# Separate score products for the first four samples, wv fetched last, and part of wk through GpSimd's queue, in a kernel of four graph layers

## The chip, the cores and the metric

The kernel runs on one core of one Trainium2 chip. The metric is the device time of one execution in microseconds (us), taken as the median of several runs; lower is better. The core's engines are named in the profile as PE (TensorE, matrix products), PEld (TensorE's weight loads), DVE (VectorE), ACT (ScalarE), POOL (GpSimd) and SP (SyncE, which issues most DMAs). Each engine executes its own instructions in order; waits between engines go by semaphores. Besides SP, ScalarE and GpSimd can issue DMAs too, each through a queue of its own.

## The reference

Everything is f32. The input is a batch of 128 samples, each of 128 nodes with 512 features, and one weighted adjacency matrix of 128 x 128 a sample. Four graph layers follow each other, each added to its input and normalised. The change lies in the first (layer 0), a diffusion over three hops with attention weights:

```python
x, adj = ...                      # [128, 128, 512], [128, 128, 128]
def L0(X, A, Wv, bv, aw, ab, Wk, bk):          # Wk: three hops, [3, 512, 512]
    Xw = X @ Wv + bv
    sj = Xw @ aw[:512, 0]
    si = Xw @ aw[512:, 0]
    e = leaky_relu(sj[:, None, :] + si[:, :, None] + ab[0], 0.2)
    alpha = A * exp(e)
    transition = alpha / (sum(alpha, -1, keepdims=True) + 1e-12)
    H, Xk = 0, X
    for k in range(3):
        H = H + Xk @ Wk[k] + bk[k]
        Xk = einsum('bij,bjd->bid', transition, Xk)
    return relu(H)
x = layernorm(x + L0(x, adj, ...))
x = layernorm(x + L1(...)); x = layernorm(x + L2(...)); x = layernorm(x + L3(...))
```

Layers 1 to 3 (hypergraph convolution through 1024 features, dense graph layer, masked attention with 8 heads) are not touched.

## The kernel before

**How it is put in order.** The body of the kernel doesn't issue instructions. Each call on `pe`, `ve` (VectorE), `ac` (ScalarE), `po` (GpSimd) or `sp` is recorded by `Plan.add` with a key (`plan.key`, the place wanted), an estimated duration (`estimate`, line 124) and its dependences. `Plan.order` (239) then plays the five engines' queues forward with these estimates, choosing at each step among the operations that could start; it has a model of the DMA path (`LANES` transfers outstanding on SP, a common `pipe`), of buffers that come free, and of the port that VectorE and GpSimd share (`shares_port`, 151). `Plan.emit` (370) does this three times, the later times with due times from `deadlines` (359), and issues everything in the planned order. So every instruction in the profile carries line 381, and groups are told apart by engine, operation and tile name. A change of a key or of one estimate can move any instruction of any engine.

**Layer 0.** `layer0` (990) handles four samples in one call, as two pairs. They are loaded (`from_dram`, tile `four`), transposed on VectorE (`turned_two`, giving `xT`), and `lefts` (809) forms the sums of blocks of `xT` on GpSimd that serve as left operands. `twice` (846) multiplies by the weights with two levels of a Strassen-Winograd scheme: seven outer steps, each a `strassen` (630) of seven products, 49 products in all for the four samples. The seven weight tiles `WT["0"]` have the name `w7`, which the profile shows as `first` together with other tiles that share the space. Each tile holds seven blocks of 128 x 386: 3 x 128 columns for the three hops, and two further columns with Wv times the two halves of `aw`, so that a product yields both the hops' inputs and the attention scores s_j and s_i (`QW = 3 * P + 2`). Results are drained from PSUM banks into `R` (tile `out`) by ScalarE and VectorE. From the two score columns of `R` the softmax is made (key `WHENT[0]`): transposes by TensorE, Prelu and Exp on ScalarE, product with `adj` on VectorE; its result `e` goes through DRAM and comes back transposed, and the two diffusion products (tile `t`) and the normalisation follow (key `WHENT[1]`). The result is written to DRAM as `x1d`.

**The start.** `prepare0` (898) makes the seven weight tiles once. It fetches `aw`, `wv` (two loads of four 128 KB DMAs on SP), the first half of the columns of `wk` for the three hops in two parts (chunks of rows `low` and `high`, on ScalarE's queue and, for two hops of `high`, on SP's), the small vectors, and the second half of `wk` on SP. TensorE broadcasts `aw` to all partitions; VectorE takes eight dot products with the rows of `wv` (`dot`, tiles `junk` and `cols0`), which are the score columns `two`. ScalarE copies the parts of `wk` and the score columns into the blocks of four tiles (B11, B21, B12, B22). `combine`, `combine_apart` and `combine_once_more` (509 to 531) form the sums of blocks and of tiles that the scheme needs, on VectorE with PSUM as one operand (`held_in_bank`, tiles `t0`, `t1` and `bank`) or on GpSimd:

```python
scores = W[j][:, :4, 0, 3 * P:]
if half:
    po.memset(scores, 0.0)
else:
    po.memset(scores[:, 2:], 0.0)
    ac.copy(scores[:, :2], two[:, 2 * g:2 * g + 2])
plan.key = COMBINE[half][g]
(combine_apart if j in (B12,) else combine)(W[j])
```

At the end it makes `c0` (the constant of the scores, from `aw_sum` and `bv_c`), the bias of the hops from `bk`, and leaves a copy of the bias in the PSUM tiles `t0` and `t1`.

Of the kernel before, what the change touches and what calls it, by code (L numbers as in the profile page):

```python
# [14 lines left out]
OP = mybir.AluOpType  # L15
AX = mybir.AxisListType

P = 128
# [25 lines left out]
LAG1, LAG2 = 1, 1.5  # L44
COMBINE = (-9, -2), (-.5, -.2), .1
SOFT = .2
PARKED, LATE = .95, 4
# [126 lines left out]
class Plan:  # L174
# [64 lines left out]
    def order(self, urgent=None):  # L239
# [41 lines left out]
        def look(e):  # L281
# [32 lines left out]
        while count < n:  # L314
# [16 lines left out]
            if o[7]:  # L331
                end = pipe = max(pipe, t + BEGIN) + o[7]
                landed += [end + LANDED] * len(o[1])
                landed = landed[-LANES:]
            if e == PE and o[8] > reached:
# [54 lines left out]
def kernel(  # L390
# [73 lines left out]
    def four():  # L464

        return tile_of("four", U, D)
# [36 lines left out]
    def held_in_bank(kind, block):  # L503

        p = tile_of(kind, QW)
        ac.copy(p, block)
        return p
# [24 lines left out]

# [365 lines left out]
    def prepare0():  # L898
        h = D // 2
        plan.key = -9.7  # L900
        awr = four().rearrange("p u f -> p (u f)")
        sp.dma_start(awr[:1], aw.rearrange("f o -> o f"), run=2 * D, parts=1)
        W = WT["0"] = [tile_of("w7", 7, 1, QW, place=(B11, B21, T2, T1, B22, T3, N4).index(k)) for k in range(7)]
        stage = [W[T2 + m].rearrange("p j o f -> p (j o f)")[:, :C * D].rearrange("p (c f) -> p c f", f=D)
                 for m in range(3)]

        def fetch(queue, dst, src, chunks, columns, run):
# [9 lines left out]

        low, high, every = slice(0, 2), slice(2, 4), slice(0, 4)
        st = [four() for _ in range(2)]
        for g, chunks in enumerate((low, high)):  # L920
            plan.key = -9.7 + .2 * g
            fetch(sp, st[g], wv0, chunks, slice(0, D), D)
        plan.key = -9
        for m in range(3):
            fetch_part(ac, m, low, 0)
        awc, bvc = fixed(2 * C, name="aw_c"), fixed(C, name="bv_c")
        ab_b, bk0b = fixed(1, name="ab_b"), row()
        with plan.together():
            for c, v, n in ((awc, aw, 2 * C), (bvc, bv0, C)):
                ac.dma_start(c, bass.AP(tensor=v.tensor, offset=v.offset, ap=[[1, P], [P, n]]), run=1)  # L930
            ac.dma_start(bk0b[:3], bk0, parts=3)
            ac.dma_start(ab_b, rows(ab, 1), run=1)
# [4 lines left out]
        awb = [bank() for _ in range(2)]  # L937
        for k in range(2):
            pe.matmul(awb[k], ones[:1], awr[:1, k * D:(k + 1) * D], start=True, stop=True)
        two = fixed(C, 2, name="cols0")  # L940
        for c in range(C):
            for k in range(2):
                dot(two[:, c, k:k + 1], st[c // 2][:, c % 2], awb[k])
        plan.key = WHEN0[0] + .05
        for m in range(3):
            fetch_part(sp, m, every, 1)
        plan.key = -9
        for g, half, j in ((0, 0, B11), (1, 0, B21), (0, 1, B12), (1, 1, B22)):
            for m in range(3):
                ac.copy(W[j][:, :4, :, m * P:(m + 1) * P].rearrange("p (n c) o i -> p c n (o i)", n=2),  # L950
                        stage[m].rearrange("p c (n i) -> p c n i", i=P)[:, 2 * g:2 * g + 2, 2 * half:2 * half + 2])
            scores = W[j][:, :4, 0, 3 * P:]
            if half:
                po.memset(scores, 0.0)
            else:
                po.memset(scores[:, 2:], 0.0)
                ac.copy(scores[:, :2], two[:, 2 * g:2 * g + 2])
            plan.key = COMBINE[half][g]
# [3 lines left out]
        combine_once_more(W)  # L962
        plan.key = -9
        p = bank()
# [7 lines left out]

        p = bank()
        pe.matmul(p, ones[:3], bk0b[:3], start=True, stop=True)
        p = p.rearrange("p (h n i) -> p h n i", h=2, n=2)
        ac.copy(bias[:, 0], p[:, 0])
        ve.tensor_tensor(bias[:, 1], p[:, 1], bias[:, 0], OP.subtract)
        plan.key = WHENT[0][0] - .1
        for kind in ("t0", "t1"):
# [10 lines left out]
    def layer0(i0):  # L990
# [16 lines left out]
        def fresh(bs):  # L1007
            def takes(d):
# [9 lines left out]

        twice(left, WT["0"], QW, lambda r, half: [R[r][:, b, 2 * half + n] for b in range(U) for n in range(2)],
              lambda r, half: [R[r][:, b, 2 * half:2 * half + 2] for b in range(U)],  # L1020
              [fresh(bias[:, half]) for half in range(2)], .28)
        yield
# [577 lines left out]
```

## Time and profile before

| what | us |
|---|---|
| median of four runs | 5377.01 |
| the four runs | 5374.19 to 5378.59 |
| the profiled execution's own time | 5374.19 |
| its span in the profile | 5372.4 |
| TensorE busy in it | 5304.7 |
| VectorE, GpSimd, ScalarE busy | 4421.8, 3909.4, 2408.9 |

The span is the time from the first to the last recorded instruction of one execution; 1.8 us lie around it. Busy times are sums of instructions' durations, and an engine that is busy for nearly the whole span, as TensorE is, need not be working at its full rate: a row of TensorE can be a product that goes slowly. The mean granted clock of TensorE over this span was 0.999 of full speed. The page's list of queues gives 806.60 MB to the queue of SP and 1.06 MB to that of ScalarE. The GpSimd queue moves nothing in the kernel before.

In answers to queries, a row of the timeline gives the start, the time it covers, the engine, line, operation, tiles (out<-in), shape and count, and in brackets the idle time ahead of it with what ended it.

### The profile page before, as it was taken

To read this page: it belongs to the slowest core of one execution; us is meant where nothing else is said; L and a number is where in the kernel's file an instruction comes from. 1 tells how busy PE (TensorE), PEld (TensorE's weight loads), DVE (VectorE), ACT (ScalarE), POOL (GpSimd) and SP (SyncE) were. 2 spreads that over 40 slices of the span, in tenths; PEclk is the share of its full clock that TensorE was granted. 3 is DMA by queue.
4 is the path that set the end of the run, shared out by engine and by line. 5 is a ranking of instruction groups with operands and counts; after the bars stand their busy time and mean duration, and the time that the engine had idled before them with its cause. 6 is when DMAs were issued, how large, how long until landed. Compare 5 with 4: busy or idle time off the path is not lost.

```text
span 5372.4 us, 92973 instructions
## 1 busy us (share of the span) xinstructions
PE 5304.7 (99%) x29039; PEld 4226.1 (79%) x29039; DVE 4421.8 (82%) x11721; ACT 2408.9 (45%) x6085; POOL 3909.4 (73%) x4937
## 2 busy tenths in 40 slices
PE   8999999999999999999999999999999999999998
PEld 4555555555888888888888889988998898889897
DVE  7788887887888888888888778888887888788776
ACT  3343343343544444444444344444444444444444
POOL 6777787676766666666666577777877777778776
PEclk9999999999999999999999999999999999999999
DMA  4444555445544554444444745555555455545543
GB/s 109 142 136 132 147 137 137 120 117 189 167 143 147 159 162 143 147 159 160 143 148 152 235 141 163 157 160 152 162 159 160 152 163 158 163 152 163 156 153 111
DMA packets 831143, 813.61 MB, mean 151 GB/s; under 512 B 258348, under 2 KB 631604, under 8 KB 830648
## 3 DMA queue, kind: packets, MB, share of 16 engines
q1 hardware_dynamic: 827650, 806.60, 49.1%
q8 instruction: 231, 3.78, 0.3%
q14 instruction: 264, 2.16, 0.1%
q10 hardware_dynamic: 2998, 1.06, 0.1%
HBM read 458.38 MB, written 349.04 MB: 150 GB/s over the span
## 4 chain that ended last, share of the span: by engine, by line
PE 87%; DVE 7%; issue 2%; DMA 1%; POOL 1%; ACT 1%; SPq 0%; ACTq 0%; DVEq 0%; POOLq 0%
PE bank L381 66%; PE t L381 21%; DVE four L381 2%; DVE out L381 1%; DVE col L381 1%; DVE junk L381 1%; DVE first L381 1%; POOL out L381 0%; SPq L381 0%; ACT out L381 0%; DVE side L381 0%; DVE rows L381 0%; POOL four L381 0%; ACT four L381 0%; DMA four<-x 0%
## 5 line engine op out<-in xcount | busy, mean ns | idle before, releaser
L381 PE MATMUL bank<-first,four 128*128 128x386 f32 (+3 forms) x6352 | 1746.9, 422 | 23.2 <-ACT first L381 9.6
L381 PEld LDWEIGHTS bank<-first,four 128*128 128x128 f32 (+2 forms) x6352 | 1088.4, 186 | 599.7 <-DVE out L381 102.5
L381 DVE TENSOR_TENSOR out<-bank,out 128x386 f32<-128x386 f32 (+1 forms) x1942 | 949.6, 508 | 249.6 <-PE bank L381 193.7
L381 DVE TENSOR_TENSOR four<-bank,four 128x256 f32<-128x256 f32 x1113 | 455.1, 417 | 150.9 <-PE bank L381 138.8
L381 POOL TENSOR_TENSOR out<-out 128x772 f32<-128x772 f32 (+3 forms) x249 | 341.8, 1383 | 271.9 <-DVE out L381 212.0
L381 POOL TENSOR_TENSOR four<-four 128x256 f32<-128x256 f32 (+2 forms) x434 | 352.1, 824 | 186.6 <-DVE four L381 140.0
L381 PE MATMUL bank<-first,out 128*128 128x256 f32 (+1 forms) x1746 | 432.3, 377 | 3.8 <-DVE four L381 1.6
L381 POOL TENSOR_TENSOR four<-four,four 128x256 f32<-128x256 f32 (+2 forms) x467 | 397.5, 856 | 10.0 <-PE bank L381 1.5
L381 POOL TENSOR_TENSOR col<-col,neghalf 128x2 f32<-128x2 f32 x320 | 228.6, 715 | 231.3 <-DVE col L381 229.6
L381 ACT COPY out<-bank 128x258 f32<-128x258 f32 (+2 forms) x489 | 195.2, 404 | 437.3 <-PE bank L381 365.2
L381 PEld LDWEIGHTS bank<-first,out 128*128 128x128 f32 (+1 forms) x1746 | 318.5, 188 | 65.4 <-issue 9.0
L381 ACT ACTIVATE four<-four,col,col 128x512 f32<-128x512 f32 (+1 forms) x355 | 308.5, 892 | 125.7 <-POOL col L381 119.9
L381 DVE TENSOR_TENSOR first<-bank,first 128x256 f32<-128x256 f32 (+1 forms) x591 | 240.8, 416 | 98.6 <-PE bank L381 89.1
L381 PE MATMUL bank<-first 128*128 128x128 f32 (+1 forms) x2132 | 297.4, 277 | 1.6 <-DVE four L381 1.6
L381 DVE BATCH_NORM_STATS2 col<-four 128x6 f32<-128x512 f32 x424 | 283.3, 682 | 10.5 <-ACT four L381 9.1
L381 ACT COPY four<-bank 128x256 f32<-128x256 f32 (+1 forms) x358 | 150.8, 424 | 302.2 <-PE bank L381 291.5
L381 PEld LDWEIGHTS bank<-first 128*128 128x128 f32 (+1 forms) x2132 | 269.7, 189 | 15.8 <-issue 3.8
L381 PE MATMUL t<-out,sq 128*128 128x512 f32 x512 | 256.3, 593 | 0.5 <-ACT t L381 0.5
L381 ACT COPY t<-out 128x512 f32<-128x512 f32 x256 | 150.9, 591 | 235.0 <-PE bank L381 83.7
L381 PE MATMUL t<-first,four 128*128 128x256 f32 (+2 forms) x1064 | 249.7, 360 | 0.6 <-DVE four L381 0.6
L381 PE MATMUL bank<-out,first 128*128 128x128 f32 (+3 forms) x1432 | 232.5, 312 | 2.2 <-DVE col L381 1.8
L381 PE MATMUL bank<-four,first 128*128 128x128 f32 (+3 forms) x1400 | 220.5, 303 | 2.4 <-DVE four L381 1.3
(526 smaller groups left out, 13154.7 us busy)
## 6 DMA issues: line engine op xcount, KB each, us to landing
h<-four SPq DMA_DIRECT2D x69, 512.0 KB, 3.3
four<-in_x_dram SPq DMA_DIRECT2D x256, 128.0 KB, 3.4
four<-h SPq DMA_DIRECT2D x64, 512.0 KB, 4.9
four<-in_x_dram SPq DMA_DIRECT2D x62, 512.0 KB, 4.6
x1d<-four SPq DMA_DIRECT2D x62, 512.0 KB, 2.9
four<-x1d SPq DMA_DIRECT2D x60, 512.0 KB, 4.6
out<-h SPq DMA_DIRECT2D x55, 512.0 KB, 5.1
h<-out SPq DMA_DIRECT2D x50, 512.0 KB, 3.2
```

What stands on the lines that cost most here:

```text
L381: call(*map(real, args), **{n: real(a) for n, a in kw.items()})
```

## The change

The kernel's three products for the hops keep their form, but the start is rearranged:

- `prepare0` fetches `bk` first. The first half of `wk` goes by chunks: the `low` ones on ScalarE's queue, the `high` ones on GpSimd's, as twelve DMAs of 64 KB. The second half stays on SP. `aw`, `wv` and the tiny vectors get the key `SCORE0` = .8 and follow on SP; `wv` is put into tiles `prep`. The broadcasts of `aw`, the eight dots and `c0` get that key too. The bias is made early.
- `WT["0"]` is filled and combined over its first 384 columns only. `score_columns` later adds the two score columns of all 49 blocks: small sums on GpSimd, copies on ScalarE.
- For the first four samples, `layer0` multiplies with 384 columns, and the scores come from 16 products of `xT` with the two columns `two`, in one bank, copied to `R` by ScalarE. The softmax of these samples gets a key not before `SCORE0 + .2`. All later samples are computed as before, with 386 columns.
- In the planner, a DMA issue on GpSimd is estimated at 1000 ns, doesn't claim the shared port, and doesn't count among SP's outstanding transfers.

```diff
@@ estimate, shares_port, order
-        return ISSUE
+        return 1000 if engine == POOL else ISSUE
-        return name != "memset"
+        return name not in ("memset", "dma_start")
-                if e == SP:
+                if ops[k][7] and e != POOL:
...
@@ weights
-        p = tile_of(kind, QW)
+        p = tile_of(kind, 3 * P)
...
-        flat = [w.rearrange("p j o f -> p (j o f)") for w in W]
         for to, a, b in ((T3, T2, B11), (N4, B21, T2)):
-            for at in (slice(0, 4 * QW), slice(4 * QW, 7 * QW)):
-                po.tensor_tensor(flat[to][:, at], flat[a][:, at], flat[b][:, at], OP.subtract)
+            for at in (slice(0, 4), slice(4, 7)):
+                po.tensor_tensor(W[to][:, at, 0], W[a][:, at, 0], W[b][:, at, 0], OP.subtract)
+
+    def score_columns(W, two):
+
+        last = lambda j: W[j][:, :, 0, 3 * P:]
+        sc = fixed(3, 7, 2, name="cols7")
+        po.memset(sc, 0.0)
+        for j in (B22, T3):
+            po.memset(last(j), 0.0)
+        for k in range(2):
+            top, low = two[:, 2 * k], two[:, 2 * k + 1]
+            ac.copy(sc[:, k, B11], top)
+            ac.copy(sc[:, k, T2], top)
+            ac.copy(sc[:, k, B21], low)
+            po.tensor_tensor(sc[:, k, T1], sc[:, k, T3], top, OP.subtract)
+            po.tensor_tensor(sc[:, k, N4], low, top, OP.subtract)
+        po.tensor_tensor(sc[:, 2], sc[:, 1], sc[:, 0], OP.subtract)
+        for j, k in ((B11, 0), (B21, 1), (T2, 0), (N4, 2)):
+            ac.copy(last(j), sc[:, k])
+        po.tensor_tensor(last(T1), last(T3), sc[:, 0], OP.subtract)
@@ prepare0
-        for m in range(3):
-            fetch_part(ac, m, low, 0)
...
-        for m in range(3):
-            fetch_part(sp if m else ac, m, high, 0)
+        for g, chunks in enumerate((slice(0, 2), slice(2, 4))):
+            plan.key = -9
+            for m in range(3):
+                fetch_part((ac, po)[g], m, chunks, 0)
+        plan.key = WHEN0[0] + .05
+        for m in range(3):
+            fetch_part(sp, m, slice(0, 4), 1)
...
+        plan.key = SCORE0
+        awr = prep()
+        sp.dma_start(awr[:1], aw.rearrange("f o -> o f"), run=2 * D, parts=1)
+        st = [prep().rearrange("p (u f) -> p u f", f=D) for _ in range(2)]
+        for g in range(2):
+            fetch(sp, st[g], wv0, slice(2 * g, 2 * g + 2), slice(0, D), D)
...
+        two = WT["cols"] = fixed(C, 2, name="cols0")
@@ layer0
+        wide = QW if i0 else 3 * P
+        twice(left, [w[:, :, :, :wide] for w in WT["0"]], wide,
...
+        if not i0:
+            two = WT["cols"]
+            plan.key = base + SCORE0 + .1
+            pt = bank()
+            with plan.together(30):
+                for r in range(2):
+                    for b in range(U):
+                        at = 2 * (U * r + b)
+                        for c in range(C):
+                            pe.matmul(pt[:, at:at + 2], xT[r][:, b, c], two[:, c], start=r == b == c == 0,
+                                      stop=c == C - 1, skip_group_check=True)
+            for r in range(2):
+                ac.copy(R[r][:, :, 0, 3 * P:], pt[:, 2 * U * r:2 * U * r + 2 * U].rearrange("p (b k) -> p b k", k=2))
+            score_columns(WT["0"], two)
+            plan.key = base
...
-            plan.key = base + WHENT[0][r]
+            plan.key = base + (WHENT[0][r] if i else max(WHENT[0][r], SCORE0 + .2))
```

In the order that the planner makes of the changed kernel, the engines' instructions differ from those of before at the start and, in places, through layer 0; after the last layer-0 samples the orders are the same.

More of the change, by code (lines that the diff above doesn't have):

```diff
@@ L45 @@
 COMBINE = (-9, -2), (-.5, -.2), .1
+SCORE0 = .8
 SOFT = .2
@@ L332, in order @@
                 end = pipe = max(pipe, t + BEGIN) + o[7]
-                landed += [end + LANDED] * len(o[1])
-                landed = landed[-LANES:]
+                if e != POOL:
+                    landed += [end + LANDED] * len(o[1])
+                    landed = landed[-LANES:]
             if e == PE and o[8] > reached:
@@ L900, in prepare0 @@
         plan.key = -9.7
-        awr = four().rearrange("p u f -> p (u f)")
-        sp.dma_start(awr[:1], aw.rearrange("f o -> o f"), run=2 * D, parts=1)
+        bk0b = row()
+        sp.dma_start(bk0b[:3], bk0, parts=3)
         W = WT["0"] = [tile_of("w7", 7, 1, QW, place=(B11, B21, T2, T1, B22, T3, N4).index(k)) for k in range(7)]
@@ L905, in prepare0 @@
                  for m in range(3)]
+        W = [w[:, :, :, :3 * P] for w in W]
         def fetch(queue, dst, src, chunks, columns, run):
@@ L916, in fetch_part @@
             fetch(queue, stage[m][:, at[0], at[1]], wk0[m], *at, h)
[L918 to L922, printed above, removed]
-        plan.key = -9
-        for m in range(3):
-            fetch_part(ac, m, low, 0)
[L926 to L932, printed above, removed]
-        for m in range(3):
-            fetch_part(sp if m else ac, m, high, 0)
+        for g, chunks in enumerate((slice(0, 2), slice(2, 4))):
[5 more added lines that the diff above has]
+            fetch_part(sp, m, slice(0, 4), 1)
+        plan.key = -9
         ones = fixed(P, name="ones")
         po.memset(ones, 1.0)
[L937 to L947, printed above, removed]
+        p = bank()
+        pe.matmul(p, ones[:3], bk0b[:3], start=True, stop=True)
+        p = p.rearrange("p (h n i) -> p h n i", h=2, n=2)
+        ac.copy(bias[:, 0], p[:, 0])
+        ve.tensor_tensor(bias[:, 1], p[:, 1], bias[:, 0], OP.subtract)
         for g, half, j in ((0, 0, B11), (1, 0, B21), (0, 1, B12), (1, 1, B22)):
@@ L951, in prepare0 @@
                         stage[m].rearrange("p c (n i) -> p c n i", i=P)[:, 2 * g:2 * g + 2, 2 * half:2 * half + 2])
[L952 to L957, printed above, removed]
             plan.key = COMBINE[half][g]
@@ L962, in prepare0 @@
         combine_once_more(W)
-        plan.key = -9
+        plan.key = SCORE0
[4 more added lines that the diff above has]
+            fetch(sp, st[g], wv0, slice(2 * g, 2 * g + 2), slice(0, D), D)
+        awc, bvc = fixed(2 * C, name="aw_c"), fixed(C, name="bv_c")
+        ab_b = fixed(1, name="ab_b")
+        with plan.together():
+            for c, v, n in ((awc, aw, 2 * C), (bvc, bv0, C)):
+                sp.dma_start(c, bass.AP(tensor=v.tensor, offset=v.offset, ap=[[1, P], [P, n]]), run=1)
+            sp.dma_start(ab_b, rows(ab, 1), run=1)
+        awb = [bank() for _ in range(2)]
+        for k in range(2):
+            pe.matmul(awb[k], ones[:1], awr[:1, k * D:(k + 1) * D], start=True, stop=True)
+        two = WT["cols"] = fixed(C, 2, name="cols0")
+        for c in range(C):
+            for k in range(2):
+                dot(two[:, c, k:k + 1], st[c // 2][:, c % 2], awb[k])
         p = bank()
@@ L971, in prepare0 @@
         ve.tensor_tensor(c0, p[:, :1], ab_b, OP.add)
[L973 to L978, printed above, removed]
+        plan.key = SCORE0
         for kind in ("t0", "t1"):
@@ L1017, in fresh @@
             return takes
-        twice(left, WT["0"], QW, lambda r, half: [R[r][:, b, 2 * half + n] for b in range(U) for n in range(2)],
-              lambda r, half: [R[r][:, b, 2 * half:2 * half + 2] for b in range(U)],
+        wide = QW if i0 else 3 * P
+        twice(left, [w[:, :, :, :wide] for w in WT["0"]], wide,
+              lambda r, half: [R[r][:, b, 2 * half + n, :wide] for b in range(U) for n in range(2)],
+              lambda r, half: [R[r][:, b, 2 * half:2 * half + 2, :wide] for b in range(U)],
               [fresh(bias[:, half]) for half in range(2)], .28)
+        if not i0:
[6 more added lines that the diff above has]
+                        at = 2 * (U * r + b)
+                        for c in range(C):
+                            pe.matmul(pt[:, at:at + 2], xT[r][:, b, c], two[:, c], start=r == b == c == 0,
[4 more added lines that the diff above has]
+            plan.key = base
         yield
```

## The prediction

> **What bounds the kernel now.** I read the page's busy shares and slices first, then the stretches of the first 70 us, then the instructions of TensorE and of the engines that release it, then the transfers.
>
> ```profile
> PE 5304.7 (99%) x29039; PEld 4226.1 (79%) x29039; DVE 4421.8 (82%) x11721; ACT 2408.9 (45%) x6085; POOL 3909.4 (73%) x4937
> ...
> PE   8999999999999999999999999999999999999998
> ```
>
> Over the whole span TensorE is the bound. Only the first slice (134 us) is below 9. In the order of the changed kernel, every engine's instructions are those of before again once the layer-0 samples are through, so what can move lies in the start-up, and in small differences of order in layer 0. The stretches of the start (columns: window, length, then busy us and count of PE, PEld, DVE, ACT, POOL, then clock, DMA share, GB/s):
>
> ```profile
> 0.00:10.00 10.00, 7.51 (x14) 3.43 (x14) 0.16 (x1) 0.31 (x1) 1.06 (x13) 1.00 0.67 147
> 10.00:20.00 10.00, 0.40 (x2) 0.37 (x2) 4.84 (x12) 5.54 (x10) 2.82 (x4) 1.00 0.79 205
> 20.00:30.00 10.00, 7.41 (x17) 3.12 (x17) 9.49 (x24) 5.91 (x15) 3.60 (x3) 1.00 1.14 209
> 30.00:40.00 10.00, 6.62 (x18) 2.72 (x17) 9.35 (x17) 5.09 (x12) 10.00 (x14) 1.00 0.87 150
> 40.00:50.00 10.00, 9.24 (x20) 3.48 (x20) 9.21 (x24) 5.65 (x14) 9.57 (x12) 0.83 0.20 52
> 50.00:60.00 10.00, 9.68 (x24) 5.00 (x24) 4.21 (x10) 1.12 (x3) 10.00 (x6) 0.83 0.11 20
> 60.00:70.00 10.00, 10.00 (x31) 5.41 (x30) 7.87 (x17) 3.58 (x7) 9.92 (x9) 1.00 0.26 74
> ```
>
> Until 30 us the transfers run at their ceiling, from 20 to 50 us VectorE is full, from 30 us on GpSimd. TensorE's busy time flatters: it issues 14 to 24 records in 10 us where it issues 31 once dense. Its own rows:
>
> ```profile
> 19.64 2.94 PE L381 MATMUL bank<-first,four 128*128 128x386 f32 x4 [9.60 <-ACT first L381]
> 28.42 5.73 PE L381 MATMUL bank<-first,four 128*128 128x386 f32 x16 [0.30 <-DVE out L381]
> 38.37 0.92 PE L381 MATMUL bank<-first,four 128*128 128x386 f32 x2 [2.37 <-DVE first L381]
> 50.20 8.44 PE L381 MATMUL bank<-first,four 128*128 128x386 f32 x20
> ```
>
> The first weight product starts at 19.64, released by ScalarE's copy of the score columns. All product rows of this view up to 58.6 us sum to 68 records, 34 products; at a dense 0.65 us each that is 22 us of work. So some 31 us of the start are lost to TensorE, and that is all that this change can touch. What releases it:
>
> ```profile
> 6.17 1.87 PE L381 MATMUL bank<-bv_c,aw_sum 128*128 128x1 f32 x8
> 16.43 0.65 DVE L381 SCALAR_TENSOR_TENSOR junk<-four,bank 128x512 f32<-128x512 f32 x1
> 16.59 1.41 POOL L381 TENSOR_TENSOR four<-four 128x256 f32<-128x256 f32 x2 [14.96 <-DVE four L381]
> 26.40 1.28 POOL L381 TENSOR_TENSOR four<-four 128x512 f32<-128x512 f32 x1 [6.91 <-DVE four L381]
> 30.18 1.14 ACT L381 COPY first<-first 128x512 f32<-128x512 f32 x2
> 46.37 6.34 POOL L381 TENSOR_TENSOR first<-first 128x1544 f32<-128x1544 f32 x2 [0.43 <-DVE first L381]
> ```
>
> To be seen: the dots on wv (16.43 is the first of eight), the operand sums of GpSimd that wait for VectorE's transposes, the last copy of wk's second half at 30.18, and the long combinations from 46.37. The transfers, 0 to 8 us and 8 to 28 us:
>
> ```profile
> DMA packets 3292, 0.98 MB, mean 122 GB/s; under 512 B 1872, under 2 KB 3284, under 8 KB 3292
> ```
> ```profile
> DMA packets 4831, 4.24 MB, mean 212 GB/s; under 512 B 660, under 2 KB 4323, under 8 KB 4831
> ...
> first<-in_L_gnn_Wk_dram SPq DMA_DIRECT2D x12, 128.0 KB, 4.3
> first<-in_L_gnn_Wk_dram ACTq DMA_DIRECT2D x6, 64.0 KB, 2.5
> ```
>
> Twice the size takes nearly twice as long to land, so what counts is bytes, not the issuing queue.
>
> **The change, part by part** (us on the end; minus is gain).
>
> 1. wv out of the front. Ahead of the end of wk's second half stand today two x loads, wv and wk: 5.0 MiB, 5.24 MB, which agrees with 0.98 + 4.24 MB by 28 us. Without wv it is 4.19 MB. At 212 GB/s, 1.05 MB are 4.9 us. The tiny loads (aw_c, bv_c, ab, 4 bytes a piece, most of the 1872 small packets) leave the front too: 0.6 more, since 0.98 MB are worth 4.6 us at 212 GB/s and took 8. Value -5.5. Ends: at the 175 GB/s of 12 to 16 us the 4.19 MB end at 3.4 + 23.9 = 27.3, -0.8; at the 234 of 16 to 20 us they end at 21.3, -6.8.
>
> 2. The eight dots. Each is 0.68 + 0.08 (read of the accumulator), 6.1 in all. Today four of them run from 16.43, four from 22.02. In the new order the first stands three combinations before the end of wk's combining and the rest among the drains of the products that follow, and TensorE's next six products each wait for a drain. VectorE is idle 5.8 us of 50 to 60: cost between 0 (cover holds) and 6.1. Most of the products behind them wait, so +4.
>
> 3. Sixteen score products with 2 columns. Nearest is the 1-column row: 1.87 / 8 = 0.234 a record, at a time when a 512-column record took 0.85 against 0.43 later, so 0.117 at full rate; two records a product. 32 x 0.117 = 3.7; at the slow rate 7.5; 0 if all fall into pauses. They stand in TensorE's order before the last product of their outer step and the softmax, so +3.7. The granted clock was 0.83 in 40 to 60 us. [...]
>
> 4. The broadcasts of aw (3.75 us, four records) and c0 (1.87) go from TensorE's idle start to between its products. Pauses there (2.37 before 38.37) hide them: 0; without that cover 2.8 at full rate.
>
> 5. 384 for 386 columns: 49 products x 2 records x 2 columns x 0.84 ns = -0.2.
>
> 6. Twelve 64 KB loads on GpSimd. Not in the trace. From below the same load on ScalarE's queue, 0.44 an issue; from above 2.5, if each held the queue until it landed. Behind them wait the operand sums, at 16.59 today; GpSimd is free from 1.5 us, so up to (16.6 - 1.4) / 12 = 1.27 an issue they cost nothing. Nearest is 0.44: 0. If the cover is gone, 12 us for each us above 1.27. [...]
>
> 7. Score columns of the weights: six small sums on GpSimd (0.2 each by the col row, 0.72 by the power row) and ten copies of 0.19 on ScalarE ahead of two output sums: 0 to 3, +0.5.
>
> 8. The softmax of the first pair started at 44.10 and its first t product at 65.9, 21.8 later. Now it starts behind the scores, near 56, while TensorE has 22 products (14 us) ahead of that t product. GpSimd's and the DMA part overlap only partly: 0 to 3, +1.
>
> Sum: -5.5 + 4 + 3.7 + 0 - 0.2 + 0 + 0.5 + 1 = +3.5. The profiled execution took 5374.2 (span 5372.4 and 1.8 around it), so 5377.7 on that scale; the median of the runs is 2.8 above it: **5380**. About 0.2% (10.8 us) is what a measurement here can tell from no change, so the likeliest case is no change. All ends together: -7.0 to +21.5, 5370 to 5398.
>
> **The rivals.**
>
> *Faster.* The start shrinks as a whole: -6.8 from the bytes, -3.4 because the slow-clock stretches (17% of 20 us) go with the pauses, and half of the 6.6 us of pauses between products (1.94, 0.35, 0.30, 0.29, 2.37, 1.19, 0.18): -13.5, 5363. For it: GpSimd's second run waits 6.91 us for a transpose that is queued behind dots, and VectorE, full from 20 to 50 us, has the dots before and after, so that moving them need cost nothing if it is VectorE's sum of work that sets this stretch. Against: 6.1 us of dots and 3.7 of scores come back at a place where TensorE waits for every drain.
>
> *Slower: GpSimd's queue.* One place, the operand sums and ScalarE's copies of wk behind the twelve issues. It decides from 1.27 us an issue, and exceeds 0.2% from 1.27 + 7.3 / 12 = 1.9. At 2.5 an issue: 12 x 1.23 = 14.8 more, 5395. For it: GpSimd executes in order and nothing shows the price; against: ScalarE's 0.44.
>
> *The transfer is hidden anyway, or wv comes too late.* wv is not last on its queue: eight x loads go before it, so it ends after 6.6 MB, at 3.4 + 31 = 34.5 plus 2 of landing, while VectorE reaches the first dot near 39. If it is later, VectorE stands, and the 5.5 gained is gone: 5386.
>
> *It doesn't do what it says.* The queue of GpSimd adds no bandwidth (212 GB/s with one queue or two); if the front is held by x's landing alone, 5383.
>
> **How the numbers follow.** Forecast 0.28, the likeliest single case but no more, since its two large terms have ends 6 us apart each; late or hidden transfer with the last rival 0.08, of which 0.07 within the bound; faster 0.25; GpSimd's queue 0.23, as nothing in the trace prices its issue; dots and scores both at their upper ends (5380 + 2.1 + 3.8 + 2.8 + 2.5 = 5391) 0.16. So faster 0.25, within 0.2% 0.28 + 0.07 = 0.35, slower 0.01 + 0.23 + 0.16 = 0.40. The range 5361 to 5398 leaves out the far part of faster and of the queue's case; the forecast's own is 5370 to 5388.
>
> **What would show it.** Right: wk's second-half copies near 25 (30.18), first product near 14, twelve POOL issues done by 16, dots between 38 and 50 with TensorE waiting for `out`, 32 short records near 51, dense from about 55. Wrong: operand sums after 17; a first dot that waits for wv; score records hidden in pauses; TensorE dense before 48; or a difference that arises after 100 us, which none of this explains.

## The result: 0.12% slower, and the profile after

| | before | after |
|---|---|---|
| median, us | 5378.73 (61 runs) | 5385.71 (41 runs) |
| ratio, 95% interval | | 1.0012 [1.0008, 1.0017] |
| span of the profiled execution | 5372.4 | 5379.6 |
| first weight product starts at | 19.64 | 15.52 |
| ninth diffusion product starts at | 90.79 | 94.88 |
| from the ninth to the 225th diffusion product | 539.7 | 543.6 |
| at half clock by the clock record, in the first 100 us | 6.83 | 13.65 |

The kernel became 7.0 us slower. The diffusion products of layer 0 (tile `t`, made from `out` and `sq`) are 512 records in both kernels, so the start times of the same one can be subtracted. The ninth comes 4.1 us later, the 225th (at 630 us before) 8.0 us later, the 512th and last (at 1350 us) 8.3, and the end of the span 7.2. So the loss has two halves: some 4 us in the first 95 us, and some 4 us in layer 0 from there to 630 us, where TensorE issues the same 1623 records in both kernels.

The stretches of the start in the changed kernel (columns as shown of before):

```profile
0.00:10.00 10.00, 0.00 (x0) 0.00 (x0) 1.00 (x1) 1.90 (x2) 7.45 (x19) 1.00 0.87 189
10.00:20.00 10.00, 5.32 (x7) 1.96 (x8) 3.50 (x8) 5.36 (x11) 2.97 (x7) 1.00 1.14 220
20.00:30.00 10.00, 8.89 (x25) 4.06 (x24) 9.29 (x21) 6.85 (x17) 9.27 (x11) 1.00 1.07 194
30.00:40.00 10.00, 7.46 (x19) 2.48 (x17) 9.84 (x23) 6.12 (x13) 7.30 (x13) 1.00 0.24 56
40.00:50.00 10.00, 9.21 (x24) 3.92 (x24) 8.90 (x22) 1.77 (x9) 10.00 (x4) 0.78 0.20 53
50.00:60.00 10.00, 10.00 (x45) 7.34 (x44) 3.04 (x8) 1.80 (x8) 4.81 (x6) 0.67 0.18 54
60.00:70.00 10.00, 10.00 (x28) 5.75 (x27) 7.28 (x18) 2.15 (x8) 8.44 (x14) 0.86 0.07 12
```

To 40 us the change does what its front half promises: 44 product records are issued by then, where before there were 34. By 60 us there are 63 against 71. The lead of ten records (3.2 us at 0.323 us each) is gone, and VectorE is again full from 20 to 50 us. The clock column is the new thing: 0.78, 0.67 and 0.86 from 40 to 70 us, where before it had 0.83, 0.83 and 1.00. Cut at the drops themselves, before and then after:

```profile
40.10:43.51 3.41, 3.04 (x5) 1.29 (x6) 3.41 (x8) 2.21 (x5) 3.41 (x7) 0.50 0.59 154
50.34:53.75 3.41, 3.41 (x6) 1.59 (x6) 0.58 (x2) 0.73 (x2) 3.41 (x3) 0.50 0.00 0
```
```profile
45.64:52.47 6.83, 6.10 (x9) 2.85 (x10) 4.70 (x13) 1.76 (x9) 6.63 (x5) 0.50 0.28 76
52.47:55.88 3.41, 3.41 (x30) 3.19 (x28) 0.95 (x3) 0.00 (x0) 1.80 (x1) 1.00 0.39 117
55.88:62.71 6.83, 6.83 (x17) 4.30 (x17) 2.29 (x9) 2.30 (x9) 3.45 (x3) 0.50 0.07 21
```

Two drops of 3.41 us have become two of 6.83. Half of what was added, 3.4 us, would be most of the 4.1 by which the start is late, if TensorE had work to do in all of it; the runs below do not bear that out. Between the two drops stands a stretch in which TensorE is busy throughout with 30 records, nearly all of them score products. Its own rows there:

```profile
46.37 6.67 PE L383 MATMUL bank<-first,four 128*128 128x384 f32 x10 [0.79 <-DVE out L383]
52.88 4.08 PE L383 MATMUL bank<-cols,four 128*128 128x2 f32 x32
56.82 1.63 PE L383 MATMUL bank<-first,four 128*128 128x384 f32 x2
58.67 7.66 PE L383 MATMUL bank<-first,four 128*128 128x384 f32 x17
```

Ten records of weight products take 6.67 us, 17 take 7.66; at 0.323 us each 17 take 5.5.

In the rest of layer 0, TensorE's waits from 100 to 600 us that the profile can name, before and then after (columns: in total, times, longest):

```profile
PE bank L381 <- DVE out L381: 0.8, 3, 0.4
PE bank L381 <- ACT out L381: 0.7, 2, 0.4
```
```profile
PE bank L383 <- ACT out L383: 1.6, 4, 0.7
PE bank L383 <- DVE out L383: 0.7, 1, 0.7
PE t L383 <- ACT t L383: 0.4, 2, 0.2
```

These are drains that come late, as before, a little more often. Summed over all intervals between TensorE's records from the ninth to the 225th diffusion product, what exceeds the records' usual spacing is some 4 us more after than before (between 9 and 10 us before, between 13 and 14 after).

### The profile page after: what moved, and what is told of

Same layout as the page of the kernel before. It is cut to its first block, busy times and chain, and to the rows that moved or that the text cites. A ratio compares the mean times of both kernels' runs of the same rounds, so it can differ in the third digit from the quotient of the medians.

```text
span 5379.6 us, 93054 instructions
## 1 busy us (share of the span) xinstructions
PE 5310.9 (99%) x29071; PEld 4230.2 (79%) x29071; DVE 4423.0 (82%) x11721; ACT 2410.4 (45%) x6095; POOL 3914.5 (73%) x4954
## 4 chain that ended last, share of the span: by engine, by line
PE 87%; DVE 7%; issue 2%; DMA 1%; ACT 1%; POOL 1%; SPq 0%; ACTq 0%; DVEq 0%; POOLq 0%
PE bank L383 67%; PE t L383 21%; DVE four L383 2%; DVE out L383 1%; DVE col L383 1%; DVE first L383 1%; DVE junk L383 1%; ACT out L383 0%; ACT four L383 0%; DVE rows L383 0%; POOL four L383 0%; DVE side L383 0%; POOL first L383 0%; SPq L383 0%; DVE bank L383 0%
## 5 line engine op out<-in xcount | busy, mean ns | idle before, releaser
L383 PE MATMUL bank<-first,four 128*128 128x386 f32 (+4 forms) x6352 | 1751.0, 423 | 16.8 <-DVE out L383 3.5
L383 DVE TENSOR_TENSOR out<-bank,out 128x386 f32<-128x386 f32 (+2 forms) x1942 | 952.0, 508 | 250.0 <-PE bank L383 197.3
L383 POOL TENSOR_TENSOR out<-out 128x772 f32<-128x772 f32 (+4 forms) x249 | 341.9, 1382 | 273.8 <-DVE out L383 209.3
L383 ACT COPY out<-bank 128x258 f32<-128x258 f32 (+3 forms) x491 | 195.4, 403 | 431.1 <-PE bank L383 354.1
L383 DVE BATCH_NORM_STATS2 col<-four 128x6 f32<-128x512 f32 x424 | 283.4, 682 | 10.6 <-ACT four L383 9.1
L383 POOL TENSOR_SCALAR sq<-sq,col 128x128 f32<-128x128 f32 x256 | 154.6, 612 | 96.9 <-DVE col L383 94.3
```

Source lines behind the costliest of these rows:

```text
L383: call(*map(real, args), **{n: real(a) for n, a in kw.items()})
```

## The experiments

Twelve kernels ran. For each the median stands beside that of the kernel before in the same comparison; the changed kernel is compared with them by its own distance to before, 7.0 us. "Start" is how much later than before the ninth diffusion product comes in its one profiled execution, "layer 0" the time from there to the 225th, "half" the time that the clock record shows at half in the first 100 us. The record has no entry before some point of the start, and up to there the column shows 1.00; but until that point the two records of a weight product start 0.64 us or more apart, which is half rate, and from it on mostly 0.32. "First" is this time, from the first weight product to the first entry, and "half" does not hold it. Before has 3.4 there. It differs by up to 6.7 us between kernels of one order, though their first products start within 1.1 us of each other, so a start is good to some 2 us (half of one drop of 3.41 us), and to some 3 where "first" differs by 6.

| kernel | median, us | before, us | ratio, 95% interval | start | first | half | layer 0 |
|---|---|---|---|---|---|---|---|
| after | 5385.71 | 5378.73 | 1.0012 [1.0008, 1.0017] | +4.1 | 2.8 | 13.65 | 543.6 |
| score1 | 5383.27 | 5379.70 | 1.0007 [0.9998, 1.0016] | +0.2 | 3.4 | 10.24 | 543.4 |
| dot2 | 5385.38 | 5379.70 | 1.0009 [1.0001, 1.0018] | +2.5 | 7.2 | 6.83 | 544.3 |
| both | 5380.66 | 5379.70 | 1.0005 [0.9996, 1.0014] | -0.9 | 9.2 | 6.83 | 542.2 |
| filler | 5386.91 | 5379.70 | 1.0015 [1.0006, 1.0023] | +7.8 | 3.6 | 10.24 | 543.8 |
| thin | 5380.73 | 5380.01 | 1.0000 [0.9991, 1.0009] | -1.4 | 9.5 | 0 | 542.7 |
| thin_g | 5376.60 | 5376.12 | 1.0001 [0.9992, 1.0010] | -1.9 | 9.2 | 6.83 | 542.7 |
| after_g | 5384.60 | 5376.12 | 1.0015 [1.0007, 1.0024] | +7.5 | 9.2 | 17.07 | 543.7 |
| sp_high | 5389.30 | 5380.01 | 1.0020 [1.0012, 1.0029] | +10.1 | 4.8 | 27.31 | 543.4 |
| wv_front | 5389.81 | 5380.01 | 1.0023 [1.0013, 1.0032] | +14.4 | 18.7 | 20.48 | 546.3 |
| early | 5395.66 | 5380.01 | 1.0030 [1.0020, 1.0041] | +14.5 | 3.0 | 23.89 | 547.0 |
| b_slack | 5364.31 | 5376.12 | 0.9978 [0.9969, 0.9986] | +1.1 | 8.0 | 6.83 | 541.2 |
| a_slack | 5373.39 | 5376.12 | 0.9990 [0.9981, 0.9999] | +9.2 | 3.6 | 23.89 | 545.4 |

"First" is to be seen in thin's stretch from 20 to 30 us: the column shows 1.00, and 22 records keep TensorE busy for 9.95 us, which at 0.323 us each would be 7.1:

```profile
20.00:30.00 10.00, 9.95 (x22) 5.03 (x22) 7.77 (x16) 6.81 (x15) 8.28 (x9) 1.00 1.04 177
```

The medians do not hang on this one execution. Drawing the recorded runs again at random, the distance to before differs from after's by -5.9 to -1.3 us for score1, -5.8 to +1.7 for dot2, -8.1 to -2.1 for both, and -1.0 to +3.6 for after_g (95%).

The first seven below `after` keep its planned order: the planner sees the full work, and only at the issue is an instruction exchanged for a smaller one (`instead` is a table that `emit` looks into).

**One score product, short dots, both, and fillers** (abridged).

```diff
+ score1: plan.instead[k] = [matmul(pt[:, :8], xT[0][:, 0, 0], two)]      # for the 16 products
+ dot2:   plan.instead[k] = [dot over out[:, :2], u[:, :2], v[:, :2]]      # for each of the eight dots
+ filler: after every second score product: matmul(pt[:, P:4 * P], xT[0][:, 0, 0], W[B11][:, 0, 0, :3 * P])
```

> The changed kernel in its own planned order, but the 16 score products are issued as one product of 8 columns, so the first four samples' scores are left out (wrong values stand in their place). Theory: the scores cost their own time and also keep TensorE's clock down, since the trace has the clock at half for 6.83 us from 45.64 and again from 55.88, the second right behind the 2-column products. Then 30 records x 0.111 = 3.3 us go, and 1.7 to 3.4 us of the second slow stretch with them: 5 to 6.7 us less than the changed kernel (5385.7), so 5379 to 5381, and the slow stretch near 55 is shorter or gone. Rival A: only their own instructions count: 3.3 less, 5382.4, the slow stretches stay 6.83 us. Rival B: the loss sits in the order of layer 0 between 100 and 560 us (the trace of after falls back by 3.4 us more there): less than 1 us is gained by the end of the start, or what is gained stays below 3.4.

The start got 3.9 us shorter (+4.1 to +0.2), the median's distance to before 3.4 us shorter (7.0 to 3.6). Theory and rival A differ by the clock: no second drop follows, so the drop behind the short records is gone, while the first drop is 3.41 us longer; the half-clock time fell only from 13.65 to 10.24. Both 3.9 and 3.4 are nearer to the 3.3 of the instructions alone than to the 5 to 6.7 of the theory. Rival B falls for the start, and layer 0 kept its 543.4.

> The changed kernel in its own planned order, but each of the eight dots on wv reads 2 of its 512 elements, so the scores are wrong. It takes some 8 x 0.6 = 4.8 us off VectorE between 38 and 48 us. Theory of the prediction (dots +4): TensorE's products there wait for drains queued behind dots, so 3 to 4 us come back: 5382. Rival: the half-rate stretch from 45.64 is caused by the pauses of this place, so it shortens by 3.41 us and 5 to 6 us come back: 5380. Rival: the wait moves to GpSimd's long combinations, 11.07 us from 39.15, which end at 50.2 whatever the dots do, and under 1.5 us comes back: 5385.

Start 1.6 us shorter, median's distance 1.3 us: within what these runs resolve the third case, though neither number is clear of none. The half-clock time fell by 6.83 us, but "first" rose by 4.4, so over both TensorE ran only 2.4 us less at half rate than in the changed kernel.

> Both of these edits in one kernel. If both costs stand on the path one behind the other: the sum, 7 to 11 us less than the changed kernel, 5375 to 5379, equal to or below the kernel before (5378.7). If the start's cost is hidden by something else and the loss is layer 0's order: above 5381. The trace at 100 us compared with before at the same diffusion product tells the start, and the growth from there to 600 us tells the order, which is that of the changed kernel in all three runs and should again be +3 to +4 us if it belongs to the order.

Start 5.0 us shorter than after, median 6.0; the sum of the two single runs is 5.5. That is less than the 7 to 11 expected of two full costs, but it adds up: dots and scores stand behind each other on the path, and together they are the whole of the start's loss. The clock has no part in this 5.0: "first" and "half" together are 16.1 us here and 16.5 in the changed kernel. Layer 0 is 542.2, still 2.5 above before.

> The changed kernel in its own planned order; among the 16 score products stand 8 more products of 384 columns into unused columns of their bank, 16 records x 0.323 = 5.2 us at full rate. Nothing is left out. Theory that the short records let the clock fall: the second slow stretch (6.83 us from 55.88) is gone or halved, which gives back 1.7 to 3.4 us: the kernel is 1.8 to 3.5 us slower than the changed one, 5387.5 to 5389. Rival, the clock has to do with something else: the slow stretch stays and the fillers cost 5.2 us or more: 5391 and up.

The eight extra products, 5.2 us at full rate, made the start 3.7 us longer, just above the expected 1.8 to 3.5. The second drop is absent:

```profile
42.99:53.23 10.24, 9.45 (x19) 4.31 (x19) 6.62 (x16) 1.77 (x9) 9.27 (x6) 0.50 0.20 51
53.23:60.05 6.82, 6.82 (x37) 4.97 (x36) 1.73 (x4) 0.00 (x0) 1.80 (x1) 1.00 0.28 79
```

The second row holds the short records with the fillers among them at full clock, and no drop follows; the median is 7.2 above before, hardly more than after's 7.0. That is the side of the clock theory, and the rival's 5391 is out; 5.2 - 3.7 = 1.5 is near half of the 3.41 us of half-clock time saved. In after, dot2 and after_g a drop follows the 32 bare short records, in wv_front one begins among them; in the run with fillers and in those with one product none does. But short records are not enough for a drop, nor needed. In sp_high, below, all 32 stand bare at full clock from 62.16 to 65.79 and no drop follows; the clock of 0.98 is the end, at 60.31, of the half-clock time before them:

```profile
60.00:70.00 10.00, 10.00 (x53) 7.16 (x53) 5.10 (x11) 2.86 (x12) 4.45 (x8) 0.98 0.21 55
```

And before and b_slack have a second drop without any short record. Point 7 below gives what the drops have in common.

**Broadcasts, c0 and GpSimd's long combinations.**

```diff
+ thin:   both, and matmul(awb[k][:, :2], ones[:1], awr[:1, k * D:k * D + 2]); of c0's four products one
+ thin_g: thin, and memset(W[to][:, at, 0], 0.0) for the four combinations of T3 and N4 on GpSimd
+ after_g: only those memsets
```

> The run with both edits (one score product, dots over 2 elements), and also: the two broadcasts of aw have 2 columns instead of 512, and of c0's four products only the first is issued; the scores are wrong. Its order is that of the changed kernel. Theory: the broadcasts and c0, which lay in TensorE's idle start before, now cost their full time between products: 4 records x (0.43 - 0.11) + 6 x 0.11 = 1.9 us at full rate, up to 3.5 where the clock is at half, so 2 to 3.5 us below the run with both edits, at the first diffusion products of the trace. Rival, the pauses there hide them (the prediction's 0): within 0.7 us of it.

0.5 us less at the start and nothing in the median: the rival. The pauses hide the broadcasts; by "first" and "half" this execution even had 6.5 us less at half rate than both, and gained no more. Without dots, scores, broadcasts and c0 the start is only 1.4 us shorter than before: that is what is left here of the gain from wv's leaving, with the later softmax and score columns in it. Where the start is held, in TensorE's and then GpSimd's rows of this run:

```profile
52.16 2.10 PE L384 MATMUL bank<-first,four 128*128 128x384 f32 x6
56.48 7.80 PE L384 MATMUL bank<-first,four 128*128 128x384 f32 x22 [2.22 <-DVE out L384]
```
```profile
40.96 11.06 POOL L384 TENSOR_TENSOR first<-first 128x1536 f32<-128x1536 f32 x4 [1.70 <-DVE first L384]
...
54.02 3.58 POOL L384 TENSOR_TENSOR out<-out 128x768 f32<-128x768 f32 x2
```

A drain on VectorE waits for GpSimd's sum of outputs, which waits behind four combinations issued in one run.

> The run with one score product, short dots, thin broadcasts and c0, and now GpSimd's four long combinations (11.06 us from 40.96 there) are memsets of the same columns, so the seven weight tiles T3 and N4 hold zeros and the outputs are wrong. Order as in the changed kernel. Theory: with the new work out of the way it is GpSimd's run of combinations, operand sums and output sums that holds TensorE (the 2.22 us pause before 56.48, released by a drain that waits 3.43 us for GpSimd's sum of outputs): that pause goes, 1.5 to 3.5 us less at the first diffusion products, 5377 to 5379. Rival: VectorE's drains and combinations hold it: within 0.7 us of the thin run.

The combinations shrank to 4.70 us and the long pause went, but the start gained only 0.5 us: in this execution the clock was at half for 6.83 us from 45.22, and in the thin run not after 25.44. The rival's number came out, but not its reason: which of GpSimd and the clock limits the stripped start stays open.

> The changed kernel with only GpSimd's four long combinations made memsets (T3 and N4 hold zeros, outputs wrong). Theory: in the changed kernel dots, scores and the half-rate stretches come after GpSimd is done (it idles 1.51 and 3.67 us between 52 and 59), so nothing is gained: within 1 us of 5385.7 and of +4.1 us at 100 us. Rival, GpSimd is the bound of the changed start as well: 2 us or more less.

Nothing was gained, the start was even 3.4 us longer. "First" and "half" together are 9.8 us longer in this execution, worth up to 4.9, so its start alone can't decide. The medians can: 8.5 us above before against 7.0 leaves no room for the rival's 2 us or more. GpSimd does not bound the changed start.

**Where the parts are fetched.** These were planned anew.

```diff
- sp_high:            fetch_part((ac, po)[g], m, chunks, 0)
+                     fetch_part((ac, sp)[g], m, chunks, 0)
+ wv_front: aw, wv, small vectors, broadcasts and dots recorded before wk's loads, at the keys of before
+ early:    aw, small vectors, c0 and the broadcasts (then ac.copy to a prep tile) at key -8.9
```

> The changed kernel, but the high chunks of wk's first half go through SP's queue instead of GpSimd's; the planner orders anew. Theory of the prediction, bytes count and not the queue: the first weight product starts within 1 us of 15.5, and the start costs the same within 1.5 us (diffusion products near +4.6 us against before at 100 us). Rival, GpSimd's queue brings the second part of wk sooner: first product 1.5 to 4 us later and the start as much longer. Rival, GpSimd's queue holds up its operand sums: the start gets shorter by 1 us or more.

```profile
11.11 7.13 PE L383 MATMUL bank<-first,four 128*128 128x384 f32 x12 [6.38 <-ACT first L383]
```

None of the three. The first product came at 11.11, 4.4 us earlier, and the start still lost 6 us more: at 30 us TensorE had done 11.2 us of work (counted at full rate) against 10.2, and from 33 to 60 us the clock was at half without a break. Until 40 us there were pauses of 0.4 to 2.8 us for VectorE's combinations and GpSimd's sums before each pair of records; from 41 us on TensorE was busy without a pause and still at half:

```profile
40.00:50.00 10.00, 10.00 (x12) 2.75 (x12) 7.42 (x20) 2.60 (x8) 9.67 (x6) 0.50 0.19 52
```

Median 9.3 us above before. An early first product is worth nothing by itself. The run does not price the queue: the planner also put x's second load behind wk's (issued from 11.62 on, in the changed kernel from 7.04), so fewer bytes stood ahead of the first product.

> The changed kernel with aw, wv, the broadcasts and the dots back at the start (keys as before), so only the separate score products, the late score columns and GpSimd's queue remain of the change. The scores' own price, 3.9 us by the run with one score product, stays; the 1.6 of the dots and the some 2.6 of broadcasts and c0 should go; but wk comes 4 to 5 us later. Theory, that wv's leaving is worth what the lead of 3.2 us at 40 us shows: 5384 to 5388, no better than the changed kernel. Rival, VectorE's sum of work sets the start and the dots fill its idle time from 10 to 20 us: 2 to 4 us better, 5381 to 5384.

Far from both numbers at the start (+14.4), and by the median (+9.8) not better than the changed kernel: moving wv back does not repair it. Since the planner chose another order, with waits of TensorE of 10.0 us in sum for VectorE's combinations from 10 to 70 us, this does not price wv's place alone. The start of +14.4 is also that of an unlucky execution: it was the slowest of the nine, 7.5 us above their median, and TensorE was at half rate until 33.26 us.

> The changed kernel with aw, its broadcasts (copied to SBUF by ScalarE), the small vectors and c0 back at the start; wv and the dots stay late. All outputs are computed. Theory: the 2.6 us of broadcasts and c0 leave the dense part and the second broadcast no longer holds the dots: 2 to 4 us less than the changed kernel, 5382 to 5384. Rival: the small loads in front cost 0.6 to 1.5 us and the dots now share SBUF reads: no gain, 5385 to 5387. The growth through layer 0 (3.4 us in the changed kernel) may take another value, since the planner orders anew; the start is read at 100 us.

The rival's side, and more than its price: 15.7 us above before. The dots, in VectorE's rows, first beside GpSimd's combinations and then with GpSimd's done:

```profile
54.79 2.17 DVE L383 SCALAR_TENSOR_TENSOR junk<-rows 128x512 f32<-128x512 f32 x1
...
59.63 0.69 DVE L383 SCALAR_TENSOR_TENSOR junk<-side,rows 128x512 f32<-128x512 f32 x1
```

With both operands in SBUF a dot took up to 2.58 us while GpSimd worked, instead of 0.69 with `aw` in PSUM; TensorE waited 9.8 us for them.

**Only the order.**

```diff
-SLACK = 60
+SLACK = 64
```

> The kernel before with nothing altered but one number of the planner (SLACK 60 to 64), so that the same work is issued in another order. Theory, that the 4 us which the changed kernel loses from the ninth to the 225th diffusion product are luck of the order: this stretch (539.7 us before, 543.6 in the changed kernel) comes out between 540.5 and 546, and the whole at 5380 to 5387, with none of the change in it. Rival, the order of layer 0 is worse because of something in the change: the stretch stays within 1 us of 539.7.

Layer 0 came out at 541.2, inside the theory's band, but only 0.5 us outside the rival's. This depends on the place: against before the run's lag wanders between 0.3 and 4.6 us over layer 0, and from the ninth to the 512th product it grows by 2.1. The whole did not come out as expected: the kernel before, with this number alone, is 11.8 us faster. The gain lies far behind the change. Records of TensorE from 3500 to 4000 us, before and then this run:

```profile
3500.00:4000.00 500.00, 496.69 (x3686) 449.49 (x3685) 403.98 (x1054) 230.31 (x783) 386.53 (x475) 1.00 0.52 159
```
```profile
3500.00:4000.00 500.00, 499.14 (x3703) 454.38 (x3702) 406.59 (x1061) 233.93 (x786) 389.87 (x479) 1.00 0.51 159
```

17 more records in 500 us, some 0.5%, in layers 2 and 3.

> The changed kernel with the same number altered (SLACK 60 to 64). Its order at the start changes too. If order is luck: the stretch from the ninth to the 225th diffusion product takes another value between 539 and 547 and the start another between +1 and +12, so the whole lies anywhere from 5380 to 5392, and may beat the kernel before only if both fall well. If the change itself sets both: within 2 us of 5385.7, with the stretch at 543.6.

The changed kernel with 64 shows the same later gain (3702 records there) and is 2.7 us below before, but has a start of +9.2 and 545.4 in layer 0. So the start and this stretch are not fixed by the change; both took other values, as the order theory said, though the whole fell below its 5380 to 5392. Both kernels beat the original before; of the two the one without the change is faster, by 9.1 us (5373.39 - 5364.31), as it was by 7.0 with 60.

## Why the prediction held, point by point

Predicted were 5380, with chances of 0.40 for slower by over 0.2%, 0.35 for no change and 0.25 for faster; measured 5385.71, slower by 0.12%, inside the range and within the bound called no change, which was not the case with the largest chance. The single forecast was +3.5 us and the measurement +7.0. The start came out as the sum said (+4.1 for +3.5), but by compensation, which is luck: dots and scores, 7.7 in the sum, came to 5.0, the broadcasts to 0.5 for 0, and all the rest, -4.2 in the sum, to -1.4. The other half came from a place that the prediction named only as what would make it wrong, a difference that arises after 100 us.

1. **wv out of the front, -5.5: too large.** The transfer part was right: the last copies of wk's second half stand at 24.78 (predicted near 25, 30.18 before), the first product at 15.52 (predicted near 14). But the step took the time of 1.05 MB for time on the end. (Its 0.6 for the tiny loads does not follow from the numbers beside it, 8 us against 4.6.) The run without scores, dots and broadcasts is 1.4 us ahead of before, one execution, while at 40 us the changed kernel's lead is 3.2 us. VectorE and GpSimd are nearly full in between, which is where the rest can have gone; no run shows that apart. The same stretches of the profile that showed VectorE above 9 of 10 us from 20 to 50 us should have capped this term.
2. **Dots, +4: 1.6** at the start (4.1 to 2.5), or 1.1 beside the shortened scores (5.0 less 3.9): under the value taken and within its ends 0 and 6.1, but hardly more than one execution resolves.
3. **Score products, +3.7: 3.9** (4.1 to 0.2). Right in size. The half-rate end of 7.5 did not apply to the records themselves, which ran at full clock (32 in 4.08 us, 0.128 each); it was the work behind them that was slowed. By the medians it is 3.4, with an interval of 1.3 to 5.9.
4. **Broadcasts and c0, 0: 0.5**, hidden as said.
5. **GpSimd's queue, 0: right**, and the rival with it refuted.

```profile
1.53 4.49 POOL L383 DMA_DIRECT2D first<-in_L_gnn_Wk_dram  x8
10.33 1.41 POOL L383 TENSOR_TENSOR four<-four 128x256 f32<-128x256 f32 x2 [1.30 <-DVE four L383]
```

In the timeline, eight issues take 4.49 us, 0.56 each, near ScalarE's 0.44 and under the 1.27 from which they would cost; the operand sums start at 10.33, released by VectorE's transpose.
6. **Softmax, +1, and score columns, +0.5.** The first diffusion product is late by 10.6 us (66.2 to 76.8), the ninth by 4.1: other products filled in. No run separates these two terms.
7. **The clock.** The sum took the score products at full rate and left their half-rate end, 7.5 for 3.7, aside. The half-clock time rose by 6.83 us, worth up to 3.4 and, with "first" 0.6 us shorter, 3.1; the run with both edits shows that the start's loss goes without it. All drops of the start here are 3.41 us long or a multiple of it. Pauses of TensorE do not stand ahead of all of them: it was busy for 0.92 and 3.42 of the 3.42 us ahead of before's two drops, and for 3.36 and 3.41 of the 3.41 us ahead of the changed kernel's, the last with short records. What the drops of these traces have in common is little work in the array, whatever the busy time. Count for each record, where it starts, 0.84 ns a column (0.323 us for 384), times the share of the 128 rows that it uses, and add this up over stretches of 3.41 us laid end to end from the clock record's first entry, in all fourteen traces to their ends. The 41 stretches at full clock that a drop follows hold 0 to 1.34 us of such work; 21,849 that none follows hold 1.29 or more, but for one with 1.18. At half clock, the 27 that a rise follows hold 1.29 or more and the 49 others 1.29 or less. The stretch before 55.88 holds 0.37, the one in sp_high with most short records (63.73) 1.53, and the one ahead of before's second drop 1.01, since products with three rows of 128 fill much of it. These are counts in this case's traces, made afterwards; at full clock the two groups overlap between 1.18 and 1.34, and no run was made to test what the counts suggest.
Of the places named to show the prediction right, the dots (37.85 to 47.57) and the issues (done by 9.02) stood where predicted or earlier and the short records (52.88) within 2 us; TensorE was not dense from 55 us but at half rate until 62.71.

8. **Layer 0, not in the sum: +4.** The failed step is the opening one, that "all that this change can touch" is the 31 us lost at the start. The small differences of order in layer 0 that it named just before got no term in the sum. The planner orders all of layer 0 anew. The seven kernels in the changed order, with starts from -1.9 to +7.8, keep 542.2 to 544.3, so it belongs to the order and not to the late start. Whether the change worsens the order or chance does stays open: the five orders planned with the change or most of it (after, sp_high, wv_front, early, a_slack) have 543.4 to 547.0, the two without it (before, b_slack) 539.7 and 541.2, which is suggestive and too few. Taken to the 512th product the picture is the same: growth of 4.2 us in after and 6.1 in a_slack, 2.1 in b_slack.

So the count is: scores and dots 5.0 together (3.9 and 1.6 taken singly), broadcasts 0.5, against 1.4 gained, +4.1 at the ninth diffusion product, a sum that closes because each run was stripped further than the one before; 4 more by the 225th; and 1 less by the end, which one pair of executions does not resolve.

## What to carry over

Moving a load out of the front paid here only until other engines were full (a lead of 3.2 us at 40 us, and 1.4 at the ninth diffusion product even without scores, dots and broadcasts); take the gain of an earlier first instruction from the instant at which the bound engine becomes dense, not from its first instruction. A busy TensorE with little work in the array fell to half clock here: with 32 tiny records in 4.08 us from 52.88, for 6.83 us from 55.88. With eight wide products among the tiny ones no drop followed; in sp_high, where they stood bare from 62.16 to 65.79, none did either. Where a planner orders everything, a change of 0.1% can't be told from another order of the same work: one number of the planner moved this kernel by 11.8 us, so compare several orders with and without the edit before crediting it.

## What the hardware showed that was not expected

- The clock column shows 1.00 from the start, but the trace's clock record has its first entry at 18.34 us in the changed kernel (15.94 to 33.26 in the fourteen traces), and until then the weight products run at half rate: their records start 0.64 us apart at 16 to 17 us, and 0.32 apart from 20 us on. The column can't be trusted before that entry.
- Stretches at half clock in the first 100 us were 3.41, 6.83, 10.24, 13.65, 17.07, 23.89 and 27.31 us long, all multiples of 3.41. The thin run had none, with a pause of 2.22 us in it. In sp_high TensorE was busy without a pause from 41.3 to 60.3 us at half clock, until 55.8 in turn with products that use 1 or 3 rows or 1 column.
- A 128 x 512 dot with two SBUF operands took 1.06 to 2.58 us beside GpSimd's combinations and sums, 0.69 without them, and 0.69 with one operand in PSUM.
- A 64 KB load issued on GpSimd cost it 0.56 us, and landed 4.8 us after its issue, as those on ScalarE's queue beside it did (4.7).
